# Layer 0's attention of a four-layer model in nine turns instead of ten, with its routing spread over four turns in twelve parts

## The chip, the cores and the metric

The kernel runs on one core of a Trainium2 chip. A core has five engines that run their own instruction lists in order and wait for each other by semaphores: TensorE (PE; matrix products and transposes, its weight loads are the row PEld), VectorE (DVE), ScalarE (ACT), GpSimd (POOL) and SyncE (SP, which here only issues transfers). The metric is the device time of one execution in microseconds.

## The reference, cut to what matters

`x` is 16 sequences of 56 tokens with 256 channels, `ctx_512` 16 sequences of 1500 with 64 channels. Four layers follow each other; each adds an attention to `ctx_512` and a feed-forward part to `x`, both behind a layer norm and a gate.

```python
# layer 0, attention: 16 heads of 16 channels; only the first 56 keys are seen, by a causal mask
qp = q @ Wq.T;  k, v = split(latent_kv @ Wkv_expand.T)
scores = einsum("bhqd,bhkd->bhqk", qh, kh) / sqrt(16)
attn = softmax(where(causal, scores, min))
x = x + tanh(g_xattn[0]) * (einsum("bhqk,bhkd->bhqd", attn, vh) @ Wout.T)
# layer 0, feed-forward: 16 experts of 176, the best 4 of each token, and a shared one of 352
probs = softmax(layernorm(x) @ Wg.T);  topk_w, sel = top_k(probs, 4)
x = x + tanh(g_ffn[0]) * (shared + sum over sel of topk_w * expert(x))
```

Layer 1 has attention over all 1500 keys and a dense 8-bit matrix, layer 2 attention and 8 experts with one chosen, layer 3 attention and 16 experts with four chosen. The change is in layer 0 alone.

## The kernel before

Tokens lie in 8 tiles of 112 (two sequences), `x[:, t, :]`. `attention_mha` works through the tiles as pairs of sequences (class `Pair`) in a software pipeline over turns `i` = 0 to 9. In turn `i` the new pair `i` gets its scores (`scores`, L509 and L515: a masked start in bfloat16 and four products a half), its maxima and differences (`shift`, L529 and L530, VectorE) and its exponentials (`exps`, L533, ScalarE). Pair `i` - 1 is transposed (`turned`, L540 on TensorE, copies L542 on ScalarE for the first half and on VectorE for the second), multiplied with the values (`values`, L549) and divided by its sums (`normalize`, L557 and L558). Pair `i` - 2 has its context transposed (`turn_context`, L563, copy L565), projected (`project`, L570) and added to `x` (`add`, L573). Near the end of a turn the next pair's keys and values are made (`keys`, L449, with four copies L452 into the one buffer `kb`; `make_values`, L458, with two copies L463 into one of two `vb`).

Between these stands the routing of the feed-forward part, for a batch of two tiles at a time: the generator `token_tiles` gives a list of parts, and `route(i, phase)` runs one part where its turn has come. The parts are: statistics of the two tiles (L1034); the inverse root by three Newton steps (L131 to L141) and the normed tokens `xr` (L1040); their transposes (L1048) and the copy to `xnT` (L1051); the logits (L1056); maximum, difference and exponential (L1059 to L1061); the probabilities `p`, comparisons of all pairs of experts (L1069 to L1072), `rank`, `sel` and the running `total`; copies of `xr` for the four choices (L1086); counts of earlier tokens (`before`, L1091 and L1093); the places (L1097 to L1102), eight scatters of token rows to DRAM (`indirect_dma_start`, L1106, issued by GpSimd) and the weights (L1113, L1114). A batch takes turns 4 to 6, 6 to 8, or 8 and 9; what is left of the third batch and the whole fourth go to `moe` as `tail`, which runs them between the first products of the shared expert (`Shared`, L1413 and L1430), makes the table of expert tiles (`table`) and then loads weights (L1197, L1198) and rows (L1204) by that table.

What sets the order: `in_order` keeps the instructions of each engine in the order of the program, so every call in the loop has a fixed place in each engine's list. PSUM buffers do the rest. `misc()` has two buffers, shared by context, projection and all routing products; `turns()` has two; keys, values and the two halves of the scores have one each. Of the routing's tiles, `xr` and `total` have two buffers, `sloti` and the others one.

GpSimd's rope (L880 to L886, five long instructions a tile) prepares the keys of layers 1 to 3. Four tiles of it are issued in turns 0 to 3. SP loads its input (L874), clears the rows that the scatters will fill (`rows<-zero`, 16 transfers, L1162) and loads the first weights of layer 1 (L231) and of the shared expert (L1397).

Of the kernel before, what the change touches and what calls it, by code (L numbers as in the profile page):

```python
# [74 lines left out]
def flamingo_kernel(ctx: ExitStack, tc: tile.TileContext, d: dict, out: bass.AP):  # L75
# [72 lines left out]
    def inverse_root_now(pool, var, n):  # L148
        root = inverse_root(pool, var, n)
        while True:  # L150
            try:
                next(root)
            except StopIteration as e:
                return e.value
# [225 lines left out]
    def attention_mha(router, roping):  # L380
        with ExitStack() as st:
# [32 lines left out]
            kb = ap1.tile([128, 4, 2, 4, S], F32, name="kb")  # L414
# [6 lines left out]
            in_order(nc.gpsimd.memset(kb, 0.0))  # L421
            in_order(nc.gpsimd.tensor_copy(identb, ident))
            in_order(nc.gpsimd.tensor_copy(maskb, bcast(mask, 1, 8)))
            in_order(nc.gpsimd.memset(qT[:, :, B * S :], 0.0))

# [19 lines left out]

            def keys(t):
                ps = ps_k.tile([128, 512], F32, name="k_ps")[:, 0 : 4 * TP].rearrange("p (q n) -> p q n", q=4)
                for q in range(4):
                    in_order(nc.tensor.matmul(ps[:, q, :], wk[:, q, :], k0d[:, 2 * t : 2 * t + 2, 0, :], start=True, stop=True))  # L449
                for h in range(4):  # L450
                    i = ps[32 * h : 32 * h + 32].rearrange("p q (b s) -> p q b s", b=2)
                    in_order(nc.scalar.copy(kb[32 * h : 32 * h + 32, :, :, h, :], i))  # L452

            def make_values(t):
                vb = vbs[t % 2]
                ps = ps_k.tile([TP, 512], F32, name="vb_ps")
                for b in range(2):
                    in_order(nc.tensor.matmul(  # L458
                        ps[:, b * D : (b + 1) * D], k0d[:, 2 * t + b].rearrange("p a s -> p (a s)"), wv, start=True, stop=True
                    ))  # L460
                pv = ps.rearrange("p (b g a c) -> p b g a c", b=2, g=H // 2, a=2)
                for a in range(2):
                    in_order(nc.scalar.activation(vb[:, :, :, 16 * a : 16 * a + 16], pv[:, :, :, a, :], AF.Copy, scale=small[0:TP, C_M + a : C_M + a + 1]))  # L463
                return vb
# [35 lines left out]
            class Pair:  # L500
# [3 lines left out]
                def scores(self):  # L504
                    t = self.t
                    self.s = []
                    for u in range(2):
                        s = ps_s.tile([128, 512], F32, name=f"s{u}_ps")
                        in_order(nc.tensor.matmul(  # L509
                            s[:, 0:448], identb, maskb.rearrange("p h s -> p (h s)"), start=True, stop=False, skip_group_check=True  # L510
                        ))
                        for q in (2 * u, 2 * u + 1):
                            for b in range(2):
                                c = t * TP + b * S
                                in_order(nc.tensor.matmul(  # L515
                                    s[64 * b : 64 * b + 64, q % 2 * 224 : q % 2 * 224 + 224],
                                    qT[:, q, c : c + 64],
                                    kb[:, q, b].rearrange("p h s -> p (h s)"),
                                    start=False,
                                    stop=True,  # L520
                                    skip_group_check=True,
                                ))
                        self.s.append(s[:, 0:448].rearrange("p (h s) -> p h s", s=S))
# [11 lines left out]
                def turned(self):  # L535
                    self.pT = ap.tile([TP, H // 2, 128], F32, name="pT0")
                    for u in range(2):
                        ps = turns()[0:TP, :].rearrange("p (g q) -> p g q", g=4)
                        for g in range(4):
                            in_order(nc.tensor.transpose(ps[:, g, :], self.p[:, u, 2 * g : 2 * g + 2, :].rearrange("p h s -> p (h s)"), ident))  # L540
                        copy = nc.scalar.copy if u == 0 else nc.vector.tensor_copy
                        in_order(copy(self.pT[:, 4 * u : 4 * u + 4, :], ps))  # L542

                def values(self):

                    self.c = misc()
                    for g in range(H // 2):
                        for b in range(2):
                            in_order(nc.tensor.matmul(  # L549
                                self.c[64 * b : 64 * b + 64, 34 * g : 34 * g + 34], self.pT[:, g, 64 * b : 64 * b + 64], self.vb[:, b, g], start=True, stop=True  # L550
                            ))
# [27 lines left out]
            def route(i, phase):  # L579

                k = i - 4 - "abc".index(phase)
                if k >= 0 and k % 2 == 0 and k // 2 < len(batches):
                    next(batches[k // 2])
# [7 lines left out]
            pairs[0].vb = make_values(0)  # L591
            norm(0)
            turn_normed(0)
            queries(0)
            norm(1)
            in_order(nc.scalar.activation(gates, gates, AF.Tanh))
            for i in range(NT + 2):
                new, turn, last = at(i), at(i - 1), at(i - 2)
                if turn:
                    turn.turned()  # L600
                if last:
                    last.turn_context()
                route(i, "a")
                if new:
                    new.scores()
                route(i, "b")
                route(i, "c")
# [3 lines left out]
                route(i, "b")  # L611
                if turn:
                    turn.values()
                if last:
                    last.project()
                if turn:
                    turn.normalize()
                if last:
                    last.add()
# [3 lines left out]
                if i + 1 < NT:  # L623
                    keys(i + 1)
                    pairs[i + 1].vb = make_values(i + 1)
                route(i, "c")
                route(i, "a")
                route(i, "b")
                route(i, "a")
                route(i, "b")  # L630
# [271 lines left out]
    class Router:  # L902
# [121 lines left out]
        def token_tiles(self, t, n):  # L1024
# [8 lines left out]
            for u in range(n):  # L1033
                in_order(nc.vector.bn_stats(st[:, u, :], x[:, t + u, :]))  # L1034
                in_order(nc.vector.bn_aggr(mv[:, u, :], st[:, u, :]))
            yield
            rstd = inverse_root_now(pool, mv[:, :, 1], n)
# [35 lines left out]
            in_order(nc.vector.tensor_reduce(rank, gt, AX.X, ALU.add))  # L1073
            in_order(nc.vector.tensor_scalar(sel, rank, float(top), None, ALU.is_lt))
# [9 lines left out]
            yield  # L1084
            for u in range(n):
                in_order(nc.scalar.copy(xr[:, u, 1:top, 0:D], bcast(xr[:, u, 0, 0:D], 1, top - 1)))  # L1086
# [78 lines left out]
    def moe(r, nxt=None, tail=None, rest=None):  # L1165
# [5 lines left out]
        with ExitStack() as st:  # L1171
# [85 lines left out]
            if l == 0:  # L1257
# [6 lines left out]
                next(last)  # L1264
                now[0][0]()
                next(before)
                next(last)
                next(last)
                next(before)
                next(last)  # L1270
                next(last)
                now[1][0]()
                next(last)
                r.table()
                next(last)
# [443 lines left out]
```

## Time and profile before

| what | value |
|---|---|
| three runs | 2392.44, 2395.82, 2396.52 us; median 2395.82 |
| the profiled execution | 2395.73 us, of which its span on the core is 2393.6 |
| busy share of the span | TensorE 94%, VectorE 64%, ScalarE 51%, GpSimd 17% |
| turn 0 of layer 0's attention starts (first scores) | 21.1 us |
| turns 1 to 9 start (first transposes of `turned`; turn 9: of the context) | 33.7, 40.2, 47.9, 55.4, 70.3, 80.6, 103.9, 114.7, 132.0 us |
| statistics of the last batch start; last routing instruction on VectorE ends | 141.3; 160.9 us |
| TensorE's shared part ends, first expert tile starts | 179.2 us |

A row of the timeline has the start in us from the span's start, the duration in us, the engine, the line in the kernel, the operation, the tiles (out, then in), the shapes (partitions x elements), how many instructions it merges, and in brackets how long the engine was idle before it and what ended that. TensorE's matmuls overlap and their ends are modelled; a product in float32 counts as two records.

### The profile page before, as it was taken

Reading aid. Unit: us, or ns where it says so; the run is one execution under the profiler, and the core shown is the slowest. Engines: PE = TensorE matmul, PEld = TensorE weight load, DVE = VectorE, ACT = ScalarE, POOL = GpSimd, SP = SyncE. Lnnn points to the kernel's source line nnn. Section 1 sums busy time; section 2 is a strip of 40 time slices with the busy share of each in tenths; the row PEclk is TensorE's granted clock in tenths of the full one; section 3 lists DMA queues with packets and bytes.
Section 4 is the critical chain, followed back from the end, with each engine's and each line's share of the span. In section 5 each row is a group of like instructions: output and inputs, shape, how many; then the busy total and the mean of one; then the engine's idle time right before and its main releaser. Section 6 shows DMA issues by size and latency. Waiting matters only on the chain. (4 is left out here: it accounts for less than half of the span.)

```text
span 2393.6 us, 47915 instructions
## 1 busy us (share of the span) xinstructions
PE 2244.0 (94%) x17842; PEld 1611.7 (67%) x17842; DVE 1531.0 (64%) x3552; ACT 1231.9 (51%) x2703; POOL 411.6 (17%) x707
## 2 busy tenths in 40 slices
PE   8678989999999999999999999979899999999697
PEld 5445655777777776447777777745577777777454
DVE  5752245778777777667777777724577777776222
ACT  4312336666666663346666666513566666665131
POOL 5454710000000002420000000001001111111233
PEclk9769989999999999989999999999899999999899
DMA  7726752000000002100000000054101000000597
GB/s 226 217 87 190 228 140 81 22 21 22 21 21 22 21 23 69 54 28 21 24 24 11 23 22 23 11 209 148 34 22 30 29 20 26 26 26 18 158 285 205
DMA packets 116676, 172.98 MB, mean 72 GB/s; under 512 B 20154, under 2 KB 78531, under 8 KB 115412
## 3 DMA queue, kind: packets, MB, share of 16 engines
q1 hardware_dynamic: 106902, 151.35, 20.6%
q0 software_dynamic: 7600, 17.14, 2.2%
q8 instruction: 144, 2.36, 0.4%
q10 hardware_dynamic: 1934, 1.34, 0.2%
q14 instruction: 96, 0.79, 0.1%
HBM read 131.24 MB, written 40.48 MB: 72 GB/s over the span
## 5 line engine op out<-in xcount | busy, mean ns | idle before, releaser
L726 ACT ACTIVATE p<-s_ps,nm 128x500 f32<-128x500 f32 x504 | 335.7, 675 | 362.7 <-DVE nm L717 362.7
L703 PE MATMUL s_ps<-kvT,qT 64*128 64x500 f32 x2016 | 485.0, 608 | 11.2 <-ACT p L735 4.6
L777 PEld LDWEIGHTS m_ps<-pT,kv 125*64 125x64 f32 x8064 | 436.7, 137 | 65.8 <-issue 57.1
L777 PE MATMUL m_ps<-pT,kv 125*64 125x128 f32 x8064 | 477.3, 275 | 1.8 <-ACT pT L770 1.2
L715 DVE TENSOR_REDUCE part<-s_ps 128x1 f32<-128x500 f32 x504 | 340.3, 677 | 214.6 <-PE s_ps L703 214.0
L703 PEld LDWEIGHTS s_ps<-kvT,qT 64*128 64x128 f32 x2016 | 186.5, 189 | 196.6 <-issue 122.7
L765 PE MATMUL m_ps<-ident,p 128*125 128x128 f32 x2016 | 297.9, 283 | 0.3
L720 DVE TENSOR_REDUCE nm<-s_ps 128x1 f32<-128x1500 f32 x168 | 287.2, 1709 | 1.9 <-PE s_ps L703 1.9
L765 PEld LDWEIGHTS m_ps<-ident,p 128*125 128x125 f32 x2016 | 248.0, 188 | 36.1 <-issue 26.6
L735 ACT ACTIVATE p<-s_ps,nm 128x1500 f32<-128x1500 f32 x168 | 254.9, 1517 | 0.8 <-DVE nm L720 0.8
L765 PE MATMUL s_ps<-ident,p 128*125 128x128 f32 x2016 | 249.5, 274 | 0.0
L746 POOL TENSOR_TENSOR den<-den 128x1 f32<-128x1 f32 x168 | 32.9, 196 | 1215.0 <-ACT p L726 1214.8
L765 PEld LDWEIGHTS s_ps<-ident,p 128*125 128x125 f32 x2016 | 234.8, 189 | 0.5
L770 ACT COPY pT<-s_ps 125x512 f32<-125x512 f32 x336 | 181.0, 596 | 99.0 <-PE s_ps L765 83.2
L770 ACT COPY pT<-m_ps 125x512 f32<-125x512 f32 x336 | 185.2, 618 | 0.0
L1223 PE MATMUL gu_ps<-wgu,xT 128*128 128x448 f32 (+2 forms) x344 | 142.9, 543 | 21.3 <-DMA wgu<-in_L_wgu 14.2
L788 DVE TENSOR_TENSOR ctxT<-m_ps,rep 64x128 f32<-64x128 f32 (+1 forms) x384 | 104.4, 272 | 89.7 <-PE m_ps L777 79.3
L1228 DVE TENSOR_TENSOR act<-gu_ps,act 128x224 f32<-128x224 f32 (+2 forms) x78 | 31.2, 401 | 187.9 <-ACT act L1227 173.5
L768 DVE COPY pT<-m_ps 125x512 f32<-125x512 f32 x168 | 116.2, 691 | 10.0 <-PE s_ps L765 0.9
L312 ACT COPY qT<-q_ps 64x224 f32<-64x224 f32 x128 | 71.8, 561 | 97.5 <-PE q_ps L356 60.3
L768 DVE COPY pT<-s_ps 125x512 f32<-125x512 f32 x168 | 114.3, 680 | 0.0
L1223 PEld LDWEIGHTS gu_ps<-wgu,xT 128*128 128x128 f32 x344 | 63.2, 194 | 72.5 <-issue 30.6
(293 smaller groups left out, 2604.6 us busy)
## 6 DMA issues: line engine op xcount, KB each, us to landing
wgu<-in_L_wgu SPq DMA_DIRECT2D x36, 448.0 KB
rows<-zero SPq DMA_DIRECT2D x16, 899.5 KB
kvT<-turned_kv SPq DMA_DIRECT2D x16, 750.0 KB
wgu<-in_L_wgu SPq DMA_DIRECT2D x34, 352.0 KB
rep<-through SPq DMA_DIRECT2D x336, 32.0 KB
xrow<-rows SPq DMA_DIRECT2D x78, 128.5 KB
wgu<-in_L_wgu SPq DMA_DIRECT2D x8, 1024.0 KB
wd<-in_L_wd SPq DMA_DIRECT2D x36, 224.0 KB
```

Of the source, the lines that this page charges most:

```text
L312: nc.scalar.copy(o, i)
L703: in_order(nc.tensor.matmul(o[:, 0 : 4 * KP], qT[64 * b : 64 * b + 64, t, j * QT : (j + 1) * QT], kvTs[t][64 * b : 64 * b + 64, z * 4 * KP ...
L715: in_order(nc.vector.tensor_reduce(self.part[:, z : z + 1], sp0[z][:, 0 : 4 * KP], AX.X, ALU.max))
L720: in_order(nc.vector.tensor_reduce(self.nm[1], sp1[:, :, 0 : 4 * KP], AX.XY, ALU.max, negate=True))
L726: in_order(nc.scalar.activation(self.p[0][:, 4 * z * KP : 4 * (z + 1) * KP], sp0[z][:, 0 : 4 * KP], AF.Exp, bias=self.nm[0], accum_out=sel ...
L735: in_order(nc.scalar.activation(self.p[1].rearrange("p (z c) -> p z c", z=3), sp1[:, :, 0 : 4 * KP], AF.Exp, bias=self.nm[1], accum_out=se ...
L765: in_order(nc.tensor.transpose(ps[:, c, :], self.p[b][:, k : k + KP], ident))
L768: in_order(nc.vector.tensor_copy(o, ps))
L770: in_order(nc.scalar.copy(o, ps))
L777: in_order(nc.tensor.matmul(self.pv[64 * b : 64 * b + 64, :], kv[:, self.t, c, b, :], self.pT[:, c, b, :], start=c == 0, stop=c == KC - 1))
L788: in_order(nc.vector.tensor_tensor(ctxs[self.t][64 * a : 64 * a + 64, b, lo - 448 * a : hi - 448 * a], self.pv[64 * b : 64 * b + 64, cols] ...
L1223: in_order(nc.tensor.matmul(ps[:, s, 0:n], xT[:, k, :], wgu[:, k, s * n : (s + 1) * n], start=k == 0, stop=k == 1))
```

## The change

The loop has nine turns. Keys are made two turns ahead and kept (copied to SBUF) one turn ahead, in two buffers `kbs`; values are made one turn ahead and kept in the pair's first turn. Making and keeping are now separate calls. A pair's context is transposed, projected and added in the same turn as its values. The copies of `turned` are a call of their own, `keep_turned`. `token_tiles` has twelve parts: each tile's statistics stand alone, the first Newton step is divided from the rest of the root, the copies of `xr` stand behind the ranks, and `sel` and `total` have a part of their own. `route(i, *phases)` runs a part for each number `k` whose batch is in its turn `k`, 2 to 5. Batch `b` so runs in turns `2b` + 2 to `2b` + 5. The order of the rest in `moe` follows from the new parts. The operations and their sizes are the same, but for one more memset on GpSimd for the second key buffer.

```diff
     def inverse_root_now(pool, var, n):
-        root = inverse_root(pool, var, n)
+        return rest_of(inverse_root(pool, var, n))
+
+    def rest_of(root):
         while True:
             try:
                 next(root)
...
-            kb = ap1.tile([128, 4, 2, 4, S], F32, name="kb")
+            kbs = [ap1.tile([128, 4, 2, 4, S], F32, name=f"kb{i}") for i in range(2)]
...
+            in_order(nc.gpsimd.memset(kbs[1], 0.0))
...
             def keys(t):
...
+                made["k", t] = ps
+
+            def keep_keys(t):
+                ps = made.pop(("k", t))
                 for h in range(4):
                     i = ps[32 * h : 32 * h + 32].rearrange("p q (b s) -> p q b s", b=2)
-                    in_order(nc.scalar.copy(kb[32 * h : 32 * h + 32, :, :, h, :], i))
+                    in_order(nc.scalar.copy(kbs[t % 2][32 * h : 32 * h + 32, :, :, h, :], i))
...
-            def route(i, phase):
-
-                k = i - 4 - "abc".index(phase)
-                if k >= 0 and k % 2 == 0 and k // 2 < len(batches):
-                    next(batches[k // 2])
+            def route(i, *phases):
+
+                for k in phases:
+                    if (i - k) % 2 == 0 and 0 <= (i - k) // 2 < len(batches):
+                        next(batches[(i - k) // 2])
...
             keys(0)
-            pairs[0].vb = make_values(0)
+            keep_keys(0)
+            make_values(0)
             norm(0)
             turn_normed(0)
+            keys(1)
             queries(0)
             norm(1)
             in_order(nc.scalar.activation(gates, gates, AF.Tanh))
-            for i in range(NT + 2):
-                new, turn, last = at(i), at(i - 1), at(i - 2)
-                if turn:
-                    turn.turned()
-                if last:
-                    last.turn_context()
-                route(i, "a")
+            for i in range(NT + 1):
+                new, cur = at(i), at(i - 1)
+                if cur:
+                    cur.turned()
+                route(i, 2, 3, 5)
+                if cur:
+                    cur.keep_turned()
+                if i + 1 < NT:
+                    keep_keys(i + 1)
+                if new:
+                    keep_values(i)
+                route(i, 4)
                 if new:
                     new.scores()
-                route(i, "b")
-                route(i, "c")
+                route(i, 3, 4)
                 if new:
                     new.shift()
                     new.exps()
-                route(i, "b")
-                if turn:
-                    turn.values()
-                if last:
-                    last.project()
-                if turn:
-                    turn.normalize()
-                if last:
-                    last.add()
+                if cur:
+                    cur.values()
+                route(i, 5)
+                if cur:
+                    cur.normalize()
+                if i + 2 < NT:
+                    keys(i + 2)
+                if cur:
+                    cur.turn_context()
+                if i + 1 < NT:
+                    make_values(i + 1)
+                route(i, 5, 3, 4, 4)
+                if cur:
+                    cur.project()
+                    cur.add()
+                route(i, 3)
                 if i == 0:
                     turn_normed(1)
                     queries(1)
-                if i + 1 < NT:
-                    keys(i + 1)
-                    pairs[i + 1].vb = make_values(i + 1)
-                route(i, "c")
-                route(i, "a")
-                route(i, "b")
-                route(i, "a")
-                route(i, "b")
                 if i < 4:
                     roping.rope(i)
...
                 in_order(nc.vector.bn_aggr(mv[:, u, :], st[:, u, :]))
-            yield
-            rstd = inverse_root_now(pool, mv[:, :, 1], n)
+                yield
+            rstd = inverse_root(pool, mv[:, :, 1], n)
+            next(rstd)
+            yield
+            rstd = rest_of(rstd)
...
             in_order(nc.vector.tensor_reduce(rank, gt, AX.X, ALU.add))
+            yield
+            for u in range(n):
+                in_order(nc.scalar.copy(xr[:, u, 1:top, 0:D], bcast(xr[:, u, 0, 0:D], 1, top - 1)))
+            yield
             in_order(nc.vector.tensor_scalar(sel, rank, float(top), None, ALU.is_lt))
...
                 before, last = tail
                 next(last)
+                next(before)
+                next(last)
+                next(before)
                 now[0][0]()
                 next(before)
-                next(last)
-                next(last)
-                next(before)
-                next(last)
-                next(last)
+                for _ in range(4):
+                    next(last)
                 now[1][0]()
-                next(last)
+                for _ in range(3):
+                    next(last)
                 r.table()
-                next(last)
                 next(last)
                 next(last)
```

## The prediction

> **What bounds the kernel now.** I read the stages first (busy time of each engine between marks), then the timelines of TensorE, VectorE and GpSimd over the first 180 us. The change touches layer 0's attention loop and the routing behind it, which ends at 160.9; all later work starts from the table and the scattered rows made there, so the change is worth what that end moves. Columns: start and end, length, busy us (instructions) of PE, PEld, DVE, ACT, POOL, then PE clock, DMA share, GB/s.
>
> ```profile
> 47.90:55.40 7.50, 7.48 (x78) 5.42 (x77) 4.15 (x8) 4.59 (x10) 0.00 (x0) 1.00 0.75 254
> 55.40:70.30 14.90, 8.29 (x81) 6.19 (x81) 12.54 (x27) 6.84 (x14) 10.69 (x5) 0.79 0.92 271
> 70.30:80.60 10.30, 10.30 (x86) 7.46 (x84) 5.80 (x13) 3.19 (x7) 3.12 (x1) 0.81 0.79 261
> 80.60:103.90 23.30, 13.34 (x87) 9.78 (x87) 19.68 (x43) 8.36 (x16) 11.86 (x10) 0.66 0.64 192
> 103.90:114.70 10.80, 8.74 (x74) 6.32 (x73) 4.06 (x9) 2.80 (x6) 5.32 (x8) 0.79 0.81 239
> 114.70:136.40 21.70, 11.86 (x74) 9.53 (x73) 12.12 (x45) 4.09 (x9) 5.99 (x7) 0.59 0.15 50
> ```
>
> A turn without routing (first line) is all TensorE, 7.5 us. Turns with routing swing between TensorE (10.3) and VectorE (14.9, 23.3; the fifth and sixth lines hold turn 7, and turns 8 and 9): routing is bunched at a turn's end, and TensorE waits for it in order. TensorE's timeline, with the idle time before in brackets, shows what follows: after 6.59 us of idling the 32 value matmuls take 1.93 us, otherwise 1.08.
>
> ```profile
> 51.39 1.08 PE L549 MATMUL m_ps<-vb,pT 112*64 112x34 f32 x32
> 69.56 0.98 PE L1048 MATMUL m_ps<-ident,xr 112*128 112x112 f32 x4 [6.59 <-DVE xr L1040]
> 90.92 0.93 PE L1091 MATMUL m_ps<-sel,small 112*112 112x16 f32 x4 [6.59 <-DVE sel L1074]
> 92.15 1.93 PE L549 MATMUL m_ps<-vb,pT 112*64 112x34 f32 x32
> ```
>
> Some of VectorE's busy time is waiting. Beside the rope on GpSimd (next fence) a comparison of 512 takes 2.24 us, alone 0.69, and a product of two numbers 1.64, alone 0.16; a reduction there keeps its 0.18.
>
> ```profile
> 64.46 1.64 DVE L140 TENSOR_TENSOR v<-v 112x2 f32<-112x2 f32 x1
> 79.20 0.18 DVE L1063 TENSOR_REDUCE sum_p<-p 112x2 f32<-112x32 f32 x1
> 81.06 2.24 DVE L1069 TENSOR_TENSOR eq<-p 112x512 f32<-112x512 f32 x1
> 115.96 0.69 DVE L1069 TENSOR_TENSOR eq<-p 112x512 f32<-112x512 f32 x1
> ```
>
> ```profile
> 77.48 3.49 POOL L880 TENSOR_TENSOR kv<-raw,cos 125x1536 f32<-125x1536 f32 x1 [9.52 <-DMA raw<-in_ctx]
> 80.94 1.81 POOL L885 TENSOR_TENSOR rot<-raw,sin 125x768 f32<-125x768 f32 x1
> 82.83 2.15 POOL L886 TENSOR_TENSOR kv<-kv,rot 125x768 f32<-125x768 f32 x1
> 85.06 2.12 POOL L885 TENSOR_TENSOR rot<-raw,sin 125x768 f32<-125x768 f32 x1
> 87.25 2.12 POOL L886 TENSOR_TENSOR kv<-kv,rot 125x768 f32<-125x768 f32 x1
> ```
>
> This rope is released by its load, on a DMA system that is 64 to 92% busy until 104; SP's queue issues the same list after the change, so I keep the ropes at 57.0 to 68.0 and 77.5 to 89.4.
>
> **The change, part by part.** VectorE's pieces, from start to next start in stretches without rope: statistics of one tile 0.55, first part of the root 1.19, second 1.18, xr 0.82, maximum and subtraction 0.40, sum to p 0.63, ranks 3.38, sel and total 0.52, places to weights 1.66; of the attention, pT copy 0.60, shift 2.43, den and ctx 0.62, add 0.40. No work is added but one memset, 1.61 us on GpSimd at 7; it delays the ones in vb from 7.3 to 8.9, which nobody reads before turn 1: nothing.
>
> Prologue: one group of key matmuls (1.1 us warm, 2.0 cold) moves ahead of the first queries and leaves turn 0, where the next pair's takes its place. ScalarE's copies of keys then bind turn 0 slightly. I put turn 1 at 34.3, against 33.7 (bounds 33.7 and 34.6): loss 0.6. The waits for kb (0.24 and 0.15) go.
>
> A plain turn: turned 0.92, scores 2.4, values 1.0, keys 1.0, then TensorE needs ctx, which VectorE has 5.4 us into the turn; TensorE is there at 5.3. So 0.15 of waiting, then 0.2 context, 1.0 values, 1.0 project: 7.67 against 7.5. ScalarE's 4.9 us fit, as copies of keys are wanted only by the next turn. Turn 3 starts at 34.3 + 2 x 7.67 = 49.64.
>
> Turn 3 (statistics, both parts of the root, xr) has 7.8 us for VectorE: xr is done at 57.55, as the rope starts; the transposes follow, turn 4 starts at 58.64. In a turn from now on VectorE has, odd: 9.97, even: 9.01 us. Turn 4: the scores wait behind the logits (0.9), shift ends 64.3, ctx 64.9; p and ranks would end at 68.9, but the rope to 68.0 lets two or three small or one large instruction through per 1.9 us: 71.3 (loss 2.4, bounds 0 and 4).
>
> Turn 5 starts on TensorE at 67.2, but VectorE owes it add, statistics, sel, the pT copy (73.4: the second half of the values waits), root and shift until 77.0, ctx 77.6. Now the third rope stands: the places (1.66) and the second half of the root (1.18) hold some nine instructions that read two SBUF operands. By the rate of the rows at 62 to 68 they end with the rope at 89, xr at 90.4 (81.3 if none collided; nearest rows are the same instructions beside a rope, so I take 90.4). TensorE has idled about 10 us, and turn 6 starts cold at 91.2.
>
> Turn 6: turned and logits at half clock 3.4, first scores at 96.4, shift 98.9, ctx 99.5, ranks 103.5; TensorE is free at 101.8. Turn 7: VectorE adds, takes statistics, sel, pT (105.6), root, shift, ctx (109.8), places (111.5), root and xr (113.5). The wait that is new stands here: `sloti` has one buffer and is written after the eight scatters of the batch before; behind it on VectorE are the root, xr and the add, and TensorE waits for these. Those scatters start once the zeroed rows have landed, which is before 96.7 (the loads behind them on the same queues are issued then) and take 8 x 1.24 + 2: done by 108.6, so it costs nothing here. Turn 8 starts at 114.1, cold: logits 117.6, values 119.4, ctx 120.1, ranks 124.1, add of the last tile 124.5 (before: the corresponding point, where the last batch's statistics begin, was 141.3).
>
> Tail: sel, half the root and the places (3.4) now stand ahead of the last batch's xr, while one statistics group less (0.6) and the shared matmuls (4.65 cold) stand between: I get the last logits 10.3 us after the add, against 7.6 after 141.3 before. From there 12.0 as before. End 124.5 + 22.3 = 146.8 against 160.9: **14.1 us earlier**. The shared weights are in by 117 (the DMA rate falls to 8 GB/s there), wanted at 127. Afterwards all moves alike: TensorE's shared part (161 to 179.2) starts from VectorE's end, the scatters (to 170.8) and first rows are not last.
>
> The profiled execution took 2395.73 (span 2393.6, 2.1 around it), the median is 2395.82: 2395.7 - 14 = **2382**.
>
> The row says that xr (a tensor_scalar over 256) runs at 0.40 us, and none lies beside a rope. [...]
>
> Turn 5 has gaps of 2.4 and 2.7 us on TensorE; the nearest row is the gap of 2.00 at 94 to 96, in a half-clock stretch that lasted on. [...]
>
> **The rivals.**
> *Milder collisions.* If only the first of the places is held (until 81.0), xr ends at 85; turn 6 starts at 85.7, warm, and turns 6 to 8 go by VectorE alone (9 + 10 + 8 = 27 to 28 instead of 33.3). The add is at 113.5, the tail 1.5 shorter: 26 us gain, 2370. The chain of scatters allows no more: 96.7 + 4 x 12.3 = 146, the last `sloti` by 134 against 160.2. For it: bursts get through between rope instructions; against: 2.24 us a comparison above.
> *The half clock stays.* TensorE's 8.4 us of a full turn are 15 at half clock (1.93 to 1.08); four such turns and a last of 10 from 58.6 end at 129 to 131, and the tail 1 us later: gain 7, 2389. For it: 90.9 to 108 stayed slow. Against: half a turn's solid work ended the slow stretch at 74.5.
> *Slower.* Context and sum now stand inside one turn, so VectorE's bunches and TensorE's work add up instead of overlapping over three turns. It decides when turns 3 to 8 average more than (160.9 + 4.8 - 22.3 - 49.6) / 6 = 15.6 us. The last six turns before averaged (141.3 - 55.4) / 6 = 14.3, one was 23.3; two like it would do: about 2403. Against: VectorE's own work is 9 to 10 a turn, and the ropes end at 89.
> *Hidden anyway.* If the first expert tiles waited for weights, not for the table, nothing would move: 2396. Against: these loads are issued from the table.
>
> **How the numbers follow.** This kernel's runs spread by 0.17%, so about 0.2% (4.8 us) can be told from no change. Forecast 0.52 (2377 to 2388), milder 0.20, half clock 0.16, slower 0.06, hidden 0.06. The range from 2370 to 2390 leaves out the last two and the tips of the bounds. Faster: 0.52 + 0.20 + 0.15 = 0.87; same 0.07; slower 0.06.
>
> **What would show it.** The add of the last tile near 124 and the table's weights loaded near 144 instead of 158; a plain turn of 7.7; long two-operand instructions on VectorE from 77 to 89; eight scatters from about 96; TensorE's idle time before the transposes of xr 8 to 10 us in turn 5 and under 4 elsewhere. Wrong would be: a wait of VectorE before `sloti`, ropes at other times, or TensorE slow all through.

## The result, and the profile after

The changed kernel takes 2398.43 us (median), the kernel before, measured with it, 2396.92: ratio 1.0002, 95% interval 0.999 to 1.0014. No change that can be measured; the forecast was 2382. Measured once more beside the experiments below it stood at 2386.48 against 2391.2, ratio 0.9983 (0.9968 to 0.9998), a gain of some 4 us. The profiled execution took 2399.29 (span 2397.5).

The stages of the changed kernel, one line a turn, turns 2 to 8 (start and end, length, busy us (instructions) of PE, PEld, DVE, ACT, POOL, then PE clock, DMA share, GB/s):

```profile
46.02:53.79 7.77, 7.68 (x77) 5.57 (x76) 4.66 (x10) 4.70 (x9) 1.48 (x1) 1.00 0.69 207
53.79:69.15 15.36, 10.48 (x81) 7.12 (x80) 14.53 (x27) 4.71 (x9) 10.98 (x7) 0.71 0.95 259
69.15:81.32 12.17, 12.17 (x87) 8.99 (x86) 7.20 (x16) 6.81 (x13) 1.57 (x1) 0.66 0.82 248
81.32:102.38 21.06, 13.16 (x87) 9.87 (x86) 18.86 (x40) 4.71 (x9) 13.17 (x9) 0.65 0.72 198
102.38:117.56 15.18, 11.11 (x78) 7.85 (x77) 8.40 (x19) 6.93 (x13) 4.88 (x7) 0.72 0.56 179
117.56:128.38 10.82, 8.76 (x78) 6.37 (x77) 9.66 (x37) 2.63 (x5) 1.88 (x2) 0.82 0.37 111
128.38:142.27 13.89, 7.81 (x56) 6.29 (x54) 5.84 (x15) 3.25 (x6) 5.92 (x8) 0.50 0.19 58
```

The plain turn is what the forecast said (7.77 against 7.67), and the turns that carry routing still swing. Turns 3 and 5, where VectorE is busy 14.5 of 15.4 and 18.9 of 21.1 us, are about as long as the worst two before (14.9 and 23.3). The timelines of VectorE and GpSimd over the same time show with what VectorE was busy:

```profile
57.19 3.55 POOL L899 TENSOR_TENSOR kv<-raw,cos 125x1536 f32<-125x1536 f32 x1 [9.69 <-DMA raw<-in_ctx]
79.75 3.61 POOL L899 TENSOR_TENSOR kv<-raw,cos 125x1536 f32<-125x1536 f32 x1 [11.34 <-DMA raw<-in_ctx]
59.81 2.69 DVE L139 TENSOR_TENSOR v<-y 112x2 f32<-112x2 f32 x1
62.73 1.64 DVE L141 SCALAR_TENSOR_TENSOR y<-v,y 112x2 f32<-112x2 f32 x1
66.47 2.09 DVE L1062 TENSOR_SCALAR xr<-x,mv,y 112x256 f32<-112x256 f32 x2
79.27 0.69 DVE L1091 TENSOR_TENSOR eq<-p 112x512 f32<-112x512 f32 x1
79.88 5.79 DVE L1092 TENSOR_TENSOR gt<-p 112x512 f32<-112x512 f32 x1
85.60 2.27 DVE L1093 TENSOR_TENSOR eq<-eq,tri 112x512 f32<-112x512 f32 x1
87.90 2.16 DVE L1094 TENSOR_TENSOR gt<-gt,eq 112x512 f32<-112x512 f32 x1
```

The third rope starts at 57.19. The second half of turn 3's root stands at 59.81, behind that moment, so xr is done at 68.56 instead of 57.55, with the rope. Turn 4, 10.5 us later than forecast by now, brings its comparisons to 79.27, where the fourth rope starts half a microsecond later: the one comparison that starts ahead of it takes its 0.69, the next 5.79. TensorE's timeline shows the price, 4.05 us ahead of the transposes of xr and 7.89 between the halves of turn 5's values, since the copy of pT stands on VectorE behind the ranks:

```profile
68.38 0.98 PE L1070 MATMUL m_ps<-ident,xr 112*128 112x112 f32 x4 [4.05 <-DVE xr L1062]
92.99 1.07 PE L563 MATMUL m_ps<-vb,pT 112*64 112x34 f32 x16 [7.89 <-DVE pT L556]
```

The end of VectorE's routing, from which all later work starts, is at 164.2 here against 160.9 before; 146.8 was forecast.

Two waits in this profile stand apart. In turn 8 (as in turn 6, for 2.45 us) VectorE waits for a group of matrix products whose last record ends at 133.5, and VectorE goes on at 137.74:

```profile
131.55 1.93 PE L563 MATMUL m_ps<-vb,pT 112*64 112x34 f32 x32
138.61 0.66 PE L577 MATMUL m_ps<-ident,ctx 128*128 128x128 f32 x2 [5.12 <-DVE sum_p L1085]
137.74 0.26 DVE L571 RECIPROCAL den<-m_ps 128x16 f32<-128x16 f32 x1 [5.66 <-remote]
```

"Remote" is a release that no record explains. The recording lacks 54 of the semaphore updates that TensorE's instructions make, and some of every other engine's; that of before, which has a smaller stop (1.61 us until 112.05), lacks 60; the recordings of the experiments lack none of TensorE's. So the first question was whether these stops belong to the change.

### The profile page after: what moved, and what is told of

The parts are those of the page before. It is cut to its first block, busy times and chain, and to the rows that moved or that the text cites. A ratio compares the mean times of both kernels' runs of the same rounds, so it can differ in the third digit from the quotient of the medians.

```text
span 2397.5 us, 47918 instructions
## 1 busy us (share of the span) xinstructions
PE 2247.8 (94%) x17837; PEld 1615.8 (67%) x17842; DVE 1533.2 (64%) x3552; ACT 1231.5 (51%) x2703; POOL 410.7 (17%) x708
## 3 DMA queue, kind: packets, MB, share of 16 engines
q1 hardware_dynamic: 106902, 151.35, 21.1%
## 5 line engine op out<-in xcount | busy, mean ns | idle before, releaser
L1246 PE MATMUL gu_ps<-wgu,xT 128*128 128x448 f32 (+2 forms) x344 | 142.0, 540 | 22.3 <-DMA wgu<-in_L_wgu 14.0
```

The lines of the kernel that those rows point to most:

```text
L1246: in_order(nc.tensor.matmul(ps[:, s, 0:n], xT[:, k, :], wgu[:, k, s * n : (s + 1) * n], start=k == 0, stop=k == 1))
```

## The experiments

Theory A: the nine turns are worth what was forecast, but the ropes on GpSimd and buffers that scatters hold took it. Theory B: the nine turns with the routing bunched in them cost as much by themselves. Theory P: the stops belong to the recording. The kernel before stood at 2389 to 2391 us beside these runs, 6 to 8 less than at first, so the ratios to it are what is compared; they differ a little from the quotients of the medians. The end of the routing is read throughout as the end of the last `weight` on VectorE's timeline, a turn's start as its first `turned` on TensorE's.

**Keys one turn ahead.** Keys and their copies leave the prologue:

```
             turn_normed(0)
-            keys(1)
             queries(0)
...
-                if i + 1 < NT:
-                    keep_keys(i + 1)
                 if new:
                     keep_values(i)
...
-                if i + 2 < NT:
-                    keys(i + 2)
+                if 0 < i < NT - 1:
+                    keys(i + 1)
                 if cur:
                     cur.turn_context()
-                if i + 1 < NT:
+                if 0 < i < NT - 1:
+                    keep_keys(i + 1)
                     make_values(i + 1)
```

(Turn 0 makes the keys and values of pair 1 after its queries.)

> The changed kernel with the keys one turn ahead again: their matmuls and copies leave the prologue, the rest of the change stays. Theory A (the loss began in the prologue, and the ropes on GpSimd multiplied it): turn 1 starts at 34 to 36 instead of 38.3, the xr of turn 3 is done before 60 instead of 68.5, TensorE starts turn 4 before 61, the last add is at 125 to 132 and the routing ends at 147 to 154 instead of 164.2: total 2384 to 2390. Theory B (the nine turns with the routing bunched in them cost this much by themselves): only the 3 to 4 us of the prologue come back, the end is at 160 or later, total 2394 or more.

Measured: 2379.9 against 2390.0, ratio 0.9952 (0.9934 to 0.9971). Turn 1 at 34.9, last add 130.1, end 152.0: as theory A has it, and the total is 4 us under its 2384 to 2390. But not by its road: xr of turn 3 was done at 68.2, turn 4 started at 68.8. VectorE's timeline shows how little was missing (GpSimd's rope starts at 57.24):

```profile
57.22 0.16 DVE L141 SCALAR_TENSOR_TENSOR y<-v,y 112x2 f32<-112x2 f32 x1
57.41 5.12 DVE L139 TENSOR_TENSOR v<-y 112x2 f32<-112x2 f32 x1
62.57 0.16 DVE L140 TENSOR_TENSOR v<-v 112x2 f32<-112x2 f32 x1
62.77 1.64 DVE L141 SCALAR_TENSOR_TENSOR y<-v,y 112x2 f32<-112x2 f32 x1
64.44 3.83 DVE L1063 TENSOR_SCALAR xr<-x,mv,y 112x256 f32<-112x256 f32 x2
```

From 57.41 the rest of root and xr would need 1.3 us; it took 10.9.

**The third and fourth rope moved** beside the experts, in the changed kernel:

```
-                if i < 4:
+                if i < 2:
                     roping.rope(i)
                     roping.load(i + 2, nc.sync)
+                if i < 4:
                     for _ in range(5):
...
-            for t in range(6, NT):
+            for t in (4, 5):
                 self.load(t, nc.sync, late)
-            for t in range(4, NT):
+            for t in range(2, NT):
                 yield from self.parts(t)
+                if t in (4, 5):
+                    self.load(t + 2, nc.sync, late)
...
-                if i % 3 == 0 and rest:
+                if i % 2 == 0 and rest:
```

> The changed kernel with the third and fourth rope taken out of the attention loop and worked off beside the experts, with those already there. Theory A: turn 1 still at 38, but xr of turn 3 by 62 instead of 68.5, ranks of turn 4 take 3.4 us instead of 11, no wait of 8 us for pT in turn 5; last add at 122 to 132 instead of 142.3, end of the routing 144 to 154; total 2378 to 2390, if the moved ropes stay hidden beside the experts. Theory B: the end stays at 158 or later and the total at 2393 or above.

Measured: 2399.1, ratio 1.0033 (1.0019 to 1.0047), but the attention did as theory A said: xr of turn 3 done at 59.4, ranks of turn 4 in 3.5 us, no wait for pT, last add 121.6, end 143.3. The total is lost later: from the end of the routing to the last expert's output 164.6 us, against 148.5 in the changed kernel. On VectorE's timeline stands something that theory A had not named:

```profile
58.66 0.73 DVE L1065 TENSOR_SCALAR xr<-x,mv,y 112x256 f32<-112x256 f32 x2
67.62 0.68 DVE L1095 TENSOR_TENSOR gt<-p 112x512 f32<-112x512 f32 x1
108.63 0.17 DVE L1128 CAST sloti<-slot 112x8 int32<-112x8 f32 x1 [8.79 <-DMA rows<-xr,sloti]
```

xr and the comparison have their own durations again. But `sloti`, which has one buffer, waits 8.79 us for the first batch's scatters, which start at 96.9 here, 19 us behind their list (77.6), and TensorE idles 9.87 us behind it. It is the wait that the forecast named, at the moment it named (108.6).

**Both together.** The two diffs above.

> The keys one turn ahead and the two ropes moved, together, in the changed kernel. Theory A: turn 1 at 34 to 36, xr of turn 3 by 58, last add at 116 to 127, end of the routing 138 to 149, total 2372 to 2385. Theory B: end 155 or later, total 2390 or more.

Measured: 2398.6, ratio 1.0035 (1.0019 to 1.0051); turn 1 at 36.5 (the first transposes of the normed inputs start at 13.50, 0.65 us later than in the first experiment), xr of turn 3 at 60.3, last add 121.1, end 143.5. The last add and the end are within theory A's limits; turn 1 and xr are half a microsecond and 2.3 us beyond them, and the moved ropes spoil the total. It is no better than the ropes alone: the same wait stands at the same place (7.36 us, until 108.14).

**The kernel before, with the same two ropes moved.**

> The kernel before with the same two ropes moved. Theory A: it loses its own collisions too (some 6 us at 62 to 68 and 5 us at 80 to 90), its routing ends at 150 to 155 instead of 160.9, total 2385 to 2391, which is 4 to 10 us behind the changed kernel with the ropes moved: the change is worth something once the ropes are out of its way. Theory B: the two kernels with the ropes moved end within 3 us of one another.

Measured: 2401.5, ratio 1.005 (1.0033 to 1.0067), end 143.4. Theory A is wrong here: without the two ropes the kernel before gains 17.5 us at the end of its routing, not 6 to 11, it then ends level with the changed one (143.3), and its total lies beyond theory A's 2385 to 2391, as the moved ropes cost time later here too. By what was on record this is theory B; but the changed kernel has 8.8 us of the new wait in its 143.3, and the kernel before has none, as it makes its places later.

**The changed kernel once more**, unchanged.

> The changed kernel as it is, once more, beside the others of this row. In its first profile TensorE stood still for 2.4 us in turn 6 (from 107.4) and for 4.2 us in turn 8 (from 133.5) with nothing in the profile that it waited for. Theory P (these stops belong to that one recording): they are gone, turn 6 takes 10 us instead of 15 and turn 8 8 to 10 instead of 14, the routing ends at 152 to 157, and the total is 1 to 7 us under that of the kernel before. Theory Q (they belong to the change): they are there again at the same two places, the end is at 162 to 166 and the total equals that of the kernel before.

Measured: ratio 0.9983 (0.9968 to 0.9998); the stops are gone, turn 6 takes 10.2 and turn 8 9.8 us, the end is at 157.0, and no semaphore update is missing. Theory P. TensorE's timeline where turn 8's stop had been:

```profile
124.52 1.91 PE L551 MATMUL t_ps<-ident,p 128*112 128x128 f32 x8
130.54 0.66 PE L577 MATMUL m_ps<-ident,ctx 128*128 128x128 f32 x2 [0.91 <-DVE sum_p L1085]
```

The two ropes meet the routing just the same (xr of turn 3 at 69.5, ranks of turn 4 done at 89.8, wait for pT 7.62). This recording is the one to hold against the forecast.

**The kernel before once more**, unchanged, for a profile.

> The kernel before, once more, for a profile beside those of this series. Its first profile had stops of TensorE too (1.1 us at 111). Theory P: they are gone and its routing ends at 158 to 161; if it ends under 157, the changed kernel has gained nothing at this place.

Measured: span 2392.1, no stops, end 161.1. So the change moved the end of the routing by 4.1 us, which agrees with the 4 us in the times.

**Ropes moved, and two lists of places.**

```
-            sloti = pool.tile([TP, 2, top], I32, name="sloti")[:, 0:n]
+            sloti = pool.tile([TP, 2, top], I32, name="sloti", bufs=2)[:, 0:n]
```

> The changed kernel with the third and fourth rope moved, as before, and a second buffer for the list of places. Theory A (once the ropes are out of the way, the wait for the first batch's scatters is what is left): VectorE's wait of 8.79 us ahead of the list of the second batch is gone, turn 8 starts at 101 to 104 instead of 111.6, the routing ends at 133 to 137 instead of 143.3, the total falls by 6 to 10 us, to 2389 to 2393. Rival (the scatters themselves bound the end, since they start at 97 in any case): the wait only moves to the scatters, the end stays at 141 or later.

Measured: ratio 1.0022 (1.0009 to 1.0035), end 141.2 instead of 143.3. The rival is right: the wait moved one step on. The scattered rows, xr, have two buffers, and the third batch's xr waits for the first batch's scatters:

```profile
108.55 0.73 DVE L1065 TENSOR_SCALAR xr<-x,mv,y 112x256 f32<-112x256 f32 x2 [8.36 <-DMA rows<-xr,sloti]
```

**Nothing in the way.** Keys one ahead, ropes moved, three lists and three xr (the room comes from a second keys buffer, which is not needed then, and from tiles that share the comparisons' memory):

```
-            sloti = pool.tile([TP, 2, top], I32, name="sloti")[:, 0:n]
+            sloti = pool.tile([TP, 2, top], I32, name="sloti", bufs=3)[:, 0:n]
...
-            xr = tmp("xr", top, DX, bufs=2)
+            xr = tmp("xr", top, DX, bufs=3)
```

> The changed kernel with the keys one turn ahead, the third and fourth rope moved beside the experts, and three lists of places and three buffers for the rows to be scattered, so that neither a rope nor a scatter can hold VectorE in the attention. Theory A (the nine turns are worth what the forecast said, 14 us, and ropes and scatters took it): turn 4 at 59 to 61, turn 6 at 80 to 82, turn 8 at 97 to 101, last add at 106 to 111, end of the routing 128 to 133, against 143.4 for the kernel before with its ropes moved. Theory B (it is worth little): end at 139 or later. The total is not the question here, since the moved ropes cost it 16 us later.

Measured: turn 4 at 60.5, turn 6 at 81.3, turn 8 at 101.9, last add 109.5, end 131.1 (total 2384.8, ratio 0.9972, 0.9955 to 0.9989, with the moved ropes' price in it). Theory A, with turn 8 less than a microsecond beyond its limit: 12.3 us ahead of the kernel before with its ropes moved, in one recording of each. Turns 3 and 4 in the view of the stages:

```profile
50.32:60.46 10.14, 9.31 (x82) 6.83 (x81) 7.60 (x26) 5.13 (x10) 0.00 (x0) 0.88 0.72 235
60.46:69.38 8.92, 8.74 (x86) 6.82 (x85) 6.92 (x17) 4.81 (x10) 0.00 (x0) 0.95 0.95 236
```

VectorE's 14.5 and 16.9 us of turn 3 in the two recordings of the changed kernel (its fourth number, 14.53, in the first fence) are 7.6 us of work.

**Ropes earlier**, with keys one ahead and two lists: three buffers for raw keys, their loads ahead of zeroed blocks.

```
-            for t in range(2):
+            for t in range(3):
                 roping.load(t, nc.sync)
...
-                    roping.load(i + 2, nc.sync)
+                    if i < 3:
+                        roping.load(i + 3, nc.sync)
```

> The changed kernel with the keys one turn ahead (and one buffer for them), with three buffers for the raw keys, so that the load of the third rope is issued ahead of the zeroed rows and the ropes run one behind the other, and with two lists of places. Theory A: ropes at 25 to 69 without a gap, xr of turn 3 done by 61, turn 4 at 59 to 62, turn 6 at 80 to 86, no wait ahead of the list of places, turn 8 at 100 to 108, last add 110 to 118, end of the routing 131 to 140, total 2360 to 2372. Rival (the load for the ropes pushes the zeroed rows back, and the first scatter with them): first scatter after 102, end 145 or later, total 2375 or more.

Measured: 2378.6, ratio 0.9946 (0.9925 to 0.9966). The third rope ran from 47.7, but the fourth waited for its load, and the zeroed blocks came later, and with them the first scatter (102.09). xr of turn 3 was done at 61.9 and turn 4 started at 65.3, both later than theory A had them. Turn 6 started at 89.0, 12 us ahead of the keys alone; then the third batch's xr waited (GpSimd and VectorE):

```profile
63.35 3.53 POOL L900 TENSOR_TENSOR kv<-raw,cos 125x1536 f32<-125x1536 f32 x1 [4.42 <-DMA raw<-in_ctx]
102.09 1.02 POOL L1130 DMA_INDIRECT rows<-xr,sloti  x1 [27.23 <-DMA wq<-in_L_wq]
116.50 0.85 DVE L1063 TENSOR_SCALAR xr<-x,mv,y 112x256 f32<-112x256 f32 x2 [8.49 <-DMA rows<-xr,sloti]
```

The end was at 149.3: the rival, for most of what the ropes had given was given back here.

**The kernel before with ropes earlier** and two lists.

> The kernel before with the same three buffers for the raw keys and the same two lists of places, without the change. Theory A (the change is worth several us once the ropes are out of its way and the list does not wait): the routing ends at 142 to 148, total 2371 to 2380, 6 to 14 us behind the changed kernel with the same. Theory B (the change is worth nothing by itself): the two are within 3 us of one another.

Measured: 2384.9, ratio 0.9973 (0.9955 to 0.999), 6.3 us behind the changed kernel with the same; but the profiled executions end their routing at 149.9 and 149.3, level, and the two intervals overlap; this end and this total are beyond theory A's limits (148 and 2380). This pair decides nothing between A and B.

**The load for the third rope later**, behind seven zeroed blocks instead of six, with keys one ahead:

```
                     roping.rope(i)
+                    if i == 0:
+                        next(clear)
                     roping.load(i + 2, nc.sync)
-                    for _ in range(5):
+                    for _ in range(4 if i == 0 else 5):
                         next(clear, None)
```

> The changed kernel with the keys one turn ahead and the load for the third rope behind seven instead of six of the zeroed blocks, so that this rope starts some 4 us later. Theory A (the forecast failed at a knife's edge: the xr of turn 3 must be made before the third rope starts): rope at 60 to 72, xr of turn 3 done at 59 to 61 instead of 68, turn 4 at 60 to 62, ranks of turn 4 end at 70 to 75, turn 6 at 90 to 94 instead of 100.6, last add 119 to 124, end of the routing 141 to 147, total 2368 to 2375. Rival (the rope takes the same 8 us wherever it falls): turn 6 at 98 or later, end 149 or later, total 2377 or more.

Measured: 2378.0, ratio 0.9943 (0.9923 to 0.9963). Timelines of GpSimd, VectorE and TensorE:

```profile
62.90 3.54 POOL L902 TENSOR_TENSOR kv<-raw,cos 125x1536 f32<-125x1536 f32 x1 [13.63 <-DMA raw<-in_ctx]
58.73 0.73 DVE L1065 TENSOR_SCALAR xr<-x,mv,y 112x256 f32<-112x256 f32 x2
61.24 1.91 PE L551 MATMUL t_ps<-ident,p 128*112 128x128 f32 x8
93.57 0.98 PE L1073 MATMUL m_ps<-ident,xr 112*128 112x112 f32 x4 [5.73 <-DVE xr L1065]
94.34 1.91 PE L551 MATMUL t_ps<-ident,p 128*112 128x128 f32 x8
```

xr of turn 3 is done 8.8 us earlier than with the keys alone, and turn 6 starts 6.4 us earlier (94.3 against 100.8). The knife's edge was real. But the ranks of turn 4 end at 76.8 and the last add stands at 127.4, beyond theory A's 75 and 124, and of the 6.4 us only 2.5 reach the end (149.5 against 152.0), so the numbers for the end and the total are the rival's. Of the other 3.9 us 3.8 lie in turns 6 and 8, where the same products took longer: with the keys alone the two halves of turn 6's scores took 0.98 us each and turn 8's values 1.13, and these turns took 9.5 and 7.9 us; here it was 1.76 and 1.21 us and 1.93, and they took 11.4 and 9.8. (1.93 is also what they took in turn 8 of both recordings of the changed kernel, at a granted clock of 0.50.)

**The load for the fourth rope right behind it.**

```
-                    for _ in range(4 if i == 0 else 5):
+                    for _ in range((0, 9, 5, 5)[i]):
```

> The same, with the load for the fourth rope directly behind that for the third, so that the two ropes run one behind the other. Theory A: ropes at 60 to 83 or so, xr of turn 3 by 61, turn 4 by 62, xr of turn 5 by 90, turn 6 at 84 to 91; then the list of the second batch waits 0 to 5 us for the first scatters, last add 113 to 122, end of the routing 135 to 144, total 2361 to 2373. Rival (the scatters, which start at 97 to 102 in any case, give it all back): end at 148 or later.

Measured: 2378.4, ratio 0.9949 (0.9929 to 0.9968); ropes from 60.5 to 84.0 with 0.7 us between them, turn 6 at 94, last add 125.1, end 147.4. Between the two theories, and no better in the total: the pair now covers the ranks of turn 4 whole (GpSimd, VectorE, TensorE):

```profile
72.47 3.54 POOL L902 TENSOR_TENSOR kv<-raw,cos 125x1536 f32<-125x1536 f32 x1
72.27 6.04 DVE L1096 TENSOR_TENSOR eq<-eq,tri 112x512 f32<-112x512 f32 x1
84.91 1.07 PE L563 MATMUL m_ps<-vb,pT 112*64 112x34 f32 x16 [11.49 <-DVE pT L556]
```

Four kernels are thus ahead of both given ones (keys one ahead, ropes earlier, the load later, the two loads paired), at ratios of 0.9943 to 0.9952 to the kernel before, where the changed one has 0.9983. What they have in common is the keys one turn ahead; from each other they can't be told.

## Why the forecast was wrong

Its points against the second recording of the changed kernel, and against the kernel with keys one ahead and the third load later, in which xr of turn 3 is done before the rope starts (its keys are not made as in the forecast):

| point | forecast | changed kernel | load later |
|---|---|---|---|
| turn 1 | 34.3 | 36.8 | 35.6 |
| turn 3 | 49.6 | 52.3 | 51.6 |
| xr of turn 3 done | 57.55 | 69.5 | 59.5 |
| turn 4 | 58.6 | 69.9 | 61.2 |
| ranks of turn 4 done | 71.3 | 89.8 | 76.8 |
| pT of turn 5 | 73.4 | 93.4 | 78.9 |
| xr of turn 5 done | 90.4 | 101.0 | 93.7 |
| turn 6 | 91.2 | 102.9 | 94.3 |
| turn 8 | 114.1 | 124.5 | 117.6 |
| last add | 124.5 | 134.3 | 127.4 |
| end of routing | 146.8 | 157.0 | 149.5 |

- *Turn 3: "xr is done at 57.55, as the rope starts".* This step failed. The forecast saw the two moments half a microsecond apart, with the rope at 57.0, and its sum costed the meeting at nothing, though it had the price of such a meeting from the rows before. With 1.3 us of VectorE's work left when the rope came, the rest took 10.9 (keys one ahead). In the second recording of the changed kernel turn 3 started 2.6 us later than forecast and the rope, at 58.46, 1.5 later, so more of the work was left. Read along the timeline, turn 4 was 11.3 us late, 8.7 of it from turn 3, and the end 10.2. In between, the fourth rope (the one at 77.5 in the forecast, which calls it the third there) fell on turn 4's ranks, which ended 18.5 us late, and not on turn 5's places and root, to which the forecast had charged it: xr of turn 5 is 10.6 late.
- *Turn 1 at 34.3, bounds to 34.6.* Wrong too: mis-sized, 2.1 us where 0.6 was charged. Leaving aside when the first inputs landed, turn 1 starts 24.1 us after the first transposes of the normed inputs (25.3 in the first recording), against 22.05 before. The forecast let the next pair's keys take the place of those that left turn 0 and charged 0.6; but three groups of keys instead of two then stand ahead of turn 1, and the one in front of the queries is cold, 2.05 us where the later ones take 1.14. With keys one ahead it is 22.0 again (22.0 to 23.3 in all kernels that have them so). And the landing itself varied: the first transposes of the normed inputs, which follow it, started at 11.7 to 13.5 in seven recordings, and the profile the forecast was made from had the earliest of them (11.68). The third rope's start varied too: 57.04 and 60.17 in the two recordings of the kernel before. An edge of half a microsecond was set against spreads of two and three.
- *Plain turn 7.67*: 7.7 to 7.8 in the changed kernel. *Tail 22.3 after the last add*: 22.7 and 22.1. *Turn 6 to the last add 33.3 us*: 31.4, and 33.1 with the load later. These held.
- *Turn 4's loss of 2.4 us in the ranks, bounds 0 and 4*: 4.7 with the load later, in whose place it was meant (8.3 instead of 3.6 us from the last product of p to the ranks' end). In the changed kernel it met the other rope and lost 6.4.
- *`sloti` waits for nothing.* It held, and only because VectorE came late. Once the ropes were away the wait stood there with 8.79 us, until 108.63, which is the forecast's own 108.6. The rival of milder collisions held that this chain allows its end of some 135 (160.9 - 26); with the ropes moved and the wait in place the end stood at 143.3.
- *The rivals.* Turns 3 to 8 averaged (134.3 - 52.3) / 6 = 13.7 us, under the 15.6 at which the change turns slower, and in the first recording 14.7. The half clock stayed for long stretches (the clock was 0.66, 0.65 and 0.50 over turns 4, 5 and 8 of the second recording) and cost something (the 3.8 us in turns 6 and 8 above), but no stretch of turns took that rival's 15 us each for it: the two longest, 3 and 5, stood on VectorE, busy 16.9 of turn 3's 17.7 us, and turns 6 to 8 took 10.2, 11.5 and 9.8. The result lies nearest to "hidden anyway" in its number, 2396, by another mechanism: the expert loads do start from the table and moved with it (issued from 154.23 in the second recording, from 158.36 in the second of before).
- *xr beside a rope.* The forecast's profile had no such row, and its sum charged the meeting nothing. Two xr of 256 took 2.09 us (first recording) and 3.83 (second recording, keys one ahead) beside the rope, 0.73 without. A comparison beside one took 5.79 and 6.04 us instead of 0.69, longer than any one of GpSimd's instructions there (3.61 and 3.54).
- *The clock.* The forecast's rows have the slow clock behind 6.59 us of idling, and it lets turn 6 start cold behind some 10. Four recordings here fell to half clock with no gap above 0.84 us in the 8 us ahead of it; see the last section.

So the record shows this. With the keys one ahead, and ropes and scatters out of its way, the schedule ends its routing 12 us ahead of the kernel before without the two ropes (131.1 against 143.4); in place it yields 4. Ropes cost the kernel before 17.7 us (161.1 to 143.4). They cost the changed one 13.7 (157.0 to 143.3), and there the scatters, from 97 on, hold it with a wait of 8.8 us; only with that wait and the prologue's keys out of the way does it reach 131.1.

Of the 10.2 us by which the end missed the forecast, taking the keys out of the prologue brought back 5.0 (152.0; 1.9 of it in turn 8, where the values took 1.13 us with the keys one ahead and 1.93 in the changed kernel), and keeping the rope off turn 3's xr another 2.5 (149.5). The last 2.7 were not taken apart further; turn 4's ranks have 2.3 of such a size, 4.7 for the forecast's 2.4. So by what they are worth at the end the prologue was the larger of the two failed steps, though the timeline shows the loss in turn 3. In the total only the first stands out, and its interval still touches that of the changed kernel (0.9952 against 0.9983); 0.9943 after both can't be told from 0.9952.

What stays open is what stopped TensorE in the first recording, and whether it also cost the executions timed with it; their ratio, 1.0002, has an interval that overlaps with that of 0.9983.

## What to carry to other kernels

Where a forecast puts the end of one stream of work within a microsecond of the start of another that blocks it, price both outcomes and look at how far the two moments scatter between executions: here a miss of under 2 us cost 9 in its turn, of which 2.5 reached the end. A gain that is set free by moving work out of the way runs into the next buffer that something later holds, so follow each freed stretch to the buffers with one or two copies before counting it. And moving one transfer by one place in a queue (seven blocks instead of six) was enough to take a rope out of xr's way, 8.8 us in that turn, without the 16 us that moving the ropes cost later; the total, 0.9943, can't be told from the 0.9952 without it.

## What the runs showed of the hardware that was not expected

TensorE's granted clock fell to half behind far less idling than the 6.59 us gaps of before. The changed kernel's stages around turn 3's context, and TensorE's timeline there:

```profile
56.80:60.20 3.40, 2.56 (x46) 2.24 (x42) 3.23 (x8) 2.01 (x4) 3.01 (x1) 1.00 1.04 303
60.20:63.60 3.40, 3.40 (x9) 2.12 (x8) 3.33 (x3) 0.46 (x2) 3.32 (x3) 0.52 1.10 263
```

```profile
57.97 1.14 PE L454 MATMUL k_ps<-k0d,wk 64*128 64x112 f32 x8
59.95 0.44 PE L577 MATMUL m_ps<-ident,ctx 128*128 128x128 f32 x2 [0.83 <-DVE ctx L572]
60.31 2.04 PE L466 MATMUL vb_ps<-wv,k0d 64*112 64x256 f32 x4
```

After 0.83 us of waiting, in a stretch in which it was busy 2.56 of 3.40 us, the clock was at half from 60.3, and the same four products took 2.04 us instead of 1.11. With the load later the same gap of 0.83 was followed by a slow stretch too (a clock of 0.56 from 59.2 to 62.9), and behind 0.84 with the keys alone and 0.83 with nothing in the way the projection took 2.05 and 2.02 us instead of 1.12. But the wait alone does not decide it. In the second recording of the changed kernel it stands at the same place (0.83 us, until 58.40), and the clock stayed full to 64.4, through a stretch with no more work in it and one with none:

```profile
57.60:61.00 3.40, 2.53 (x10) 1.44 (x10) 3.30 (x6) 1.30 (x2) 2.54 (x1) 1.00 0.96 282
61.00:64.40 3.40, 0.00 (x0) 0.00 (x0) 3.30 (x4) 0.00 (x0) 3.32 (x3) 1.00 1.08 261
```

With the two loads paired the wait is there too (0.83 us, until 58.33), and all products from there to 73.4 took their short times (the four behind it 1.11 us, the projection 1.12). What tells the two cases apart was not found, so a schedule can't count on the clock after such a wait, nor on losing it.

Small instructions were held beside a rope as well: with the keys one ahead a product of 112x2 took 0.16 us at 62.57, where it started between two of GpSimd's instructions, and 5.12 at 57.41, where one of GpSimd's had started at 57.24.
